# Routing of the first half sequence in five stages less, and a thinner first turn of experts

## The chip, the cores and the metric

The kernel runs on one core of a Trainium2 chip. The metric is the device time of one execution in microseconds; the time before is 976.54, the median of three executions (974.52, 976.54 and 977.25). The engines are named as the profile names them: PE (TensorE, with its weight loads as PEld), DVE (VectorE), ACT (ScalarE), POOL (GpSimd) and SP, which issues most DMAs.

## The reference, cut to what matters

Four sequences of 1024 tokens with 256 channels pass a linear attention with 16 heads, and then a mixture of eight experts. Each token takes its two best experts; each expert takes at most 320 tokens of a sequence, in token order, so the place of a token depends on how many tokens before it chose the same expert.

```python
x = x + attn(layernorm(x))                       # 16 heads of 16, recurrent state over chunks
h = layernorm(x)
probs = softmax(h @ gate_w.T)                    # 8 experts
_, chosen = top_k(probs, 2)
count = cumsum(one_hot(chosen), axis=tokens)     # per sequence and expert
kept = count <= 320                              # the capacity of one expert in one sequence
x = x + sum over kept of probs * (silu(h @ w1[e]) * (h @ w3[e])) @ w2[e]
```

## The kernel before, in words

**Blocks and stages.** The attention goes over 16 blocks of 256 tokens, four to a sequence. For each block the loop at L1091 runs 15 stages; every stage advances a few generators by one step, so one stage is a small piece of PE work. I count the stages through: stage 58 is the thirteenth of the fourth block. `front` makes the projections of a block one to two blocks ahead, `chunk` the scores (tile `pa`, masked by DVE into `aw`) and the outputs (tile `y`) of 128 tokens, `back` the group normalisation (a chain of DVE instructions on `var`, `rah`, `ryh`), the gate (`zT`) and the output projection (`po`), which DVE adds to `x`.

**Order.** PE keeps the order in which the program issues (`manual_schedule`). The other engines' queues are ordered by a scheduler that works from its own estimates. Each queue runs strictly in its order.

**Routing.** When half a sequence of 512 tokens has gone through `back`, the generator `routed` is put in line. Each stage advances it by two steps, so a step that yields without work delays what follows by half a stage. `logits` normalises the rows into the tile `hs`, transposes them on PE (`trh`), multiplies by the gate (`pl`), transposes the result back (`plt`) and copies it to `lg`. `route` picks the two experts by small DVE instructions on 128x32 elements (`mx`, `d`, `cand`, `sel`), adds up the choices within a partition (`before`, L742), lets PE add over partitions and count (the two matmuls of `pcnt`, L751 and L754), and makes the row numbers `is` and the weights in `hs` by some fifteen more small DVE instructions (L758 to L809). Then POOL scatters the rows of `hs` to a buffer `disp` in DRAM, one DMA of 128 rows at a time (L815): eight for the first half sequence. Segment 0 is the first half of sequence 0, segment 1 its second half, segments 2 to 4 whole sequences.

**Experts.** The expert work is a generator `work` that yields after each small piece and tells how many columns it streamed. There are four turns of eight experts. In the first turn every expert has one tile of 128 rows, all from segment 0; it may begin `LAGS[0]` = 8 stages after segment 0 is routed. An expert loads its weights and its rows `xe` from `disp` (SP, L863), transposes them (`pe`, L884), makes seven hidden pieces (`p`, L915, then ACT's silu and DVE's product `act`, L904), and the result (`pw`, L936), which POOL adds to the output in DRAM (L943). After each stage a credit grows by `RATES[turn]` columns, and expert pieces are issued until it is used up.

**Constants.** Stages 1 to 240 carry attention. After them only experts remain. `AFTER` = (0, 2, 3, 4) tells which segment must be routed before each turn. POOL also computes `xx` (L407), a part of the mixes `xm_g` (L453, L457) and the recurrent state (L559, L561), all in the same queue as the scatters.

Of the kernel before, what the change touches and what calls it, by code (L numbers as in the profile page):

```python
# [40 lines left out]
AFTER = (0, 2, 3, 4)  # L41
# [9 lines left out]

FIRST = 5

RATES = (455, 1470, 1400, 1400)

LAGS = (8, 5, 4, 4)

# [8 lines left out]
def rwkv_then_moe_kernel(  # L66
# [24 lines left out]
    def bank(tag, name):  # L91
        return ps.tile(
            [P, 512], F32, tag=tag, name=name, bufs={"m": 4, "y": 1, "f": 3}[tag])
# [12 lines left out]
    def rows(ap, b, r):  # L106
        i = b * T + r * RB
        return ap[i:i + RB, :].rearrange("(t p) c -> p t c", p=P)
# [220 lines left out]
    def norm_stats(key, src, nm, t0=0, n=RT, behind=None, by_rows=False):  # L329

        ve = sm.tile([P, n], F32, tag=f"ve{n}", name=f"ve{nm}", bufs=2)
        nb = sm.tile([P, n], F32, tag=f"nb{n}", name=f"nb{nm}", bufs=2)
        if by_rows:
            st = sm.tile([P, n, 6], F32, tag="st", name=f"st{nm}", bufs=2)
            mv = sm.tile([P, n, 2], F32, tag="mv", name=f"mv{nm}", bufs=2)
            for t in range(n):
                nc.vector.bn_stats(st[:, t, :], src[:, t0 + t, :])
                nc.vector.bn_aggr(mv[:, t, :], st[:, t, :])
                yield
            mean, sign = mv[:, :, 0], -1.0  # L340
            nc.vector.tensor_scalar(ve, mv[:, :, 1], LN_EPS, ROOT, ALU.add, ALU.mult)
        else:

            mean, sign = sm.tile([P, n], F32, tag="mn", name=f"mn{nm}", bufs=2), 1.0
            for t in range(n):
                with tc.issue_after(behind) if behind else nullcontext():
                    nc.scalar.activation(  # L347
                        aside, src[:, t0 + t, :], AF.Copy, scale=-1.0 / C,
                        accum_out=mean[:, t:t + 1])
                nc.scalar.activation(  # L350
                    aside, src[:, t0 + t, :], AF.Square, bias=mean[:, t:t + 1],
                    accum_out=ve[:, t:t + 1])
                yield
            nc.vector.tensor_scalar(ve, ve, ROOT / C, LN_EPS * ROOT, ALU.mult, ALU.add)
        rs, parts = rsqrt(ve, n, nm)
        parts[0]()
        yield
        parts[1]()
        last["nb"] = nc.vector.scalar_tensor_tensor(
            nb, mean, sign, rs, ALU.mult, ALU.mult).ins  # L360
        stats[key] = rs, nb, t0
# [5 lines left out]
    def normed(dst, src, key, t):  # L367
        rs, nb, t0 = stats[key]
        t -= t0
        return nc.scalar.activation(  # L370
            dst, src, AF.Identity, bias=nb[:, t:t + 1], scale=rs[:, t:t + 1])
# [245 lines left out]
    def segment_of(b, r):  # L617
        return next(g for g, (sb, t0, nt) in enumerate(SEGMENTS)
                    if sb == b and t0 <= r * RT < t0 + nt)

    def logits(b, r):

        nm = f"{b}_{r}"
        nc.sync.dma_start(out=rows(out, b, r), in_=xb[b, r])
        yield from norm_stats(("f", b, r), xb[b, r], f"f{nm}")
        yield
        hs = a2.tile([P, RT, W], F32, tag="hs", name=f"hs{nm}")
        nc.gpsimd.iota(
            hs.bitcast(I32)[:, :, C:C + 1], pattern=[[P, RT], [0, 1]], base=b * T + r * RB,
            channel_multiplier=1)  # L630
        for t in range(RT):
            normed(hs[:, t, :C], xb[b, r][:, t, :], ("f", b, r), t)
            if t == TPB - 1:
                yield
        g = segment_of(b, r)
        t0 = r * RT - SEGMENTS[g][1]
        if t0 == 0:
            last["hs"] = []
            last["lg"] = sm.tile([P, SEGMENTS[g][2], E], F32, tag="lg", name=f"lg{g}", bufs=2)
        last["hs"].append(hs)  # L640
        yield from (None,) * (6 if g < AFTER[1] else 2)

        hTs = []
        for u in range(RT // TPB):
            pt = bank("m", f"trh{nm}_{u}")
            for cc in range(CC):
                for i in range(TPB):
                    nc.tensor.transpose(
                        pt[:, cc * TB + i * P:cc * TB + (i + 1) * P],
                        hs[:, u * TPB + i, cc * P:(cc + 1) * P], ident)  # L650
            hT = a1.tile([P, CC, TB], F32, tag="hT", name=f"hT{nm}_{u}", bufs=2)
            nc.scalar.copy(hT.rearrange("p cc i -> p (cc i)"), pt)
            hTs.append(hT)
            yield
        yield from (None,) * 3
        pl = bank("m", f"pl{nm}")
        for cc in range(CC):
            for t in range(RT):
                u, i = divmod(t, TPB)
                nc.tensor.matmul(  # L660
                    pl[32 * t:32 * t + 32, :P], gt[:, cc, :], hTs[u][:, cc, i * P:(i + 1) * P],
                    start=cc == 0, stop=cc == CC - 1, tile_position=(0, 32 * t),
                    skip_group_check=True,
                )
        lgT = sm.tile([P, P], F32, tag="lgT", name=f"lgT{nm}")
        nc.scalar.copy(lgT, pl[:, :P])
        yield from (None,) * 3
        pg = bank("m", f"plt{nm}")
        nc.tensor.transpose(pg[:, :P], lgT, ident)
        nc.scalar.copy(  # L670
            last["lg"][:, t0:t0 + RT, :],
            pg[:, :P].rearrange("p (t e) -> p t e", t=RT)[:, :, :E])
        yield from (None,) * 2

    def route(g):
# [70 lines left out]
                earlier[:, 1:, :], earlier[:, 1:, :],  # L746
                last["earlier"].unsqueeze(1).to_broadcast([P, nt, E]), ALU.add)
        last["earlier"] = earlier[:, nt, :]
        yield from (None,) * (2 if g == AFTER[-1] else 8)
        pc = bank("m", f"pcnt{nm}")  # L750
        nc.tensor.matmul(  # L751
            pc[:, :(nt + 1) * E], ones, flat(earlier), start=True, stop=False,
# [264 lines left out]
    def routed(b, r):  # L1017
        yield from logits(b, r)
        g = segment_of(b, r)
        if (r + 1) * RT == SEGMENTS[g][1] + SEGMENTS[g][2]:  # L1020
            yield from route(g)
            clock.routed[g] = clock.step
# [67 lines left out]
    with tc.manual_schedule(engines={ENG.PE}):  # L1090
        for n in range(NBLK):  # L1091
# [13 lines left out]
            for i, stage in enumerate((  # L1105
# [19 lines left out]
                clock.step += 1  # L1125
                credit = min(credit + RATES[clock.turn], 4 * RATES[clock.turn])

# [74 lines left out]
```

## Time and profile before

| | |
|---|---|
| median of three executions | 976.54 us (974.52 to 977.25) |
| the profiled execution | 978.46 us, of which the span on the core is 976.7 us |
| PE busy | 944.2 us (97%) |
| DVE busy | 447.0 us (46%), but 18.47 of 20 us at 80 to 100 us |
| ACT, POOL busy | 320.1 us (33%), 244.6 us (25%) |
| mean granted PE clock | 0.988 |

A row of the windows view gives, for a stretch of time in us, the busy time of PE, PEld, DVE, ACT and POOL with the number of instructions, then the granted PE clock, the share of DMA and the GB/s. A row of the timeline gives start, duration, engine, source line, operation, tiles and count; the square bracket holds the idle time before it and what ended it. All times count from the start of the span.

### The profile page before, as it was taken

The numbers are of one execution on the slowest core, as the hardware profiler recorded it, in microseconds if no ns is written. First come the engines' busy times: TensorE is split into PE (matmuls) and PEld (weight loads), VectorE is DVE, ScalarE is ACT, GpSimd is POOL, SyncE is SP. The second block draws the span as 40 slices with busy tenths as digits, with TensorE's granted clock in tenths as the row PEclk, the third lists the DMA queues.
The fourth block names the chain that finished last, engine by engine and source line by source line (L and its number), as shares of the span: only waits on it lengthen the run. The fifth ranks groups of instructions, "written<-read, shape, count | busy, mean of one in ns | idle before, by whom it ended". The sixth has DMA issues, their size and how long they took to land. (4 is left out here: it accounts for less than half of the span.)

```text
span 976.7 us, 17096 instructions
## 1 busy us (share of the span) xinstructions
PE 944.2 (97%) x6754; PEld 749.7 (77%) x6754; DVE 447.0 (46%) x1303; ACT 320.1 (33%) x811; POOL 244.6 (25%) x265
## 2 busy tenths in 40 slices
PE   7989899999999999999999999999999999999995
PEld 6766678878787788888788778888866866767664
DVE  7888766656676634445443434322221222222221
ACT  8647544743654531524214124111111111111110
POOL 5321513312227212121452111541111110211111
PEclk9999999989999999999999999999999999999998
DMA  5997224514446444353465545785645234433421
GB/s 162 245 252 244 84 95 142 184 60 141 153 125 219 153 124 136 93 153 89 128 192 151 153 135 157 208 248 168 175 123 153 76 87 147 135 94 92 147 54 19
DMA packets 92073, 139.06 MB, mean 142 GB/s; under 512 B 5456, under 2 KB 73552, under 8 KB 91984
## 3 DMA queue, kind: packets, MB, share of 16 engines
q1 hardware_dynamic: 79120, 120.36, 39.2%
q0 software_dynamic: 12720, 17.47, 9.7%
q8 instruction: 58, 0.95, 0.4%
q14 instruction: 31, 0.25, 0.1%
q10 hardware_dynamic: 144, 0.02, 0.0%
HBM read 103.45 MB, written 34.39 MB: 141 GB/s over the span
## 5 line engine op out<-in xcount | busy, mean ns | idle before, releaser
L915 PE MATMUL p<-xeT,w 128*128 128x256 f32 (+2 forms) x1960 | 430.8, 374 | 2.8 <-DVE act L904 1.5
L915 PEld LDWEIGHTS p<-xeT,w 128*128 128x128 f32 x1960 | 328.4, 191 | 94.8 <-issue 10.5
L920 ACT ACTIVATE sl<-p 128x256 f32<-128x256 f32 (+2 forms) x245 | 91.2, 375 | 486.6 <-PE p L915 479.1
L904 DVE TENSOR_TENSOR act<-sl,p 128x256 f32<-128x256 f32 (+2 forms) x245 | 99.5, 408 | 284.2 <-ACT sl L920 168.4
L943 POOL DMA_INDIRECT y_out<-ye,xe x67 | 105.3, 1571 | 478.0 <-DVE ye L940 448.1
L936 PE MATMUL pw<-w,act 128*128 128x256 f32 x938 | 211.9, 381 | 0.3 <-DVE act L904 0.3
L936 PEld LDWEIGHTS pw<-w,act 128*128 128x128 f32 x938 | 174.9, 190 | 24.6 <-DVE act L904 1.0
L940 DVE TENSOR_SCALAR ye<-pw,xe 128x256 f32<-128x256 f32 x67 | 32.1, 483 | 138.6 <-PE pw L936 138.5
L510 DVE TENSOR_TENSOR aw<-pa,wmat 128x512 f32<-128x512 f32 x128 | 79.4, 683 | 11.4 <-PE pa L502 11.3
L815 POOL DMA_INDIRECT disp<-hs,is x64 | 63.7, 996 | 44.3 <-issue 15.4
L423 PE MATMUL pc<-xm,wa 128*128 128x256 f32 x264 | 67.1, 400 | 5.9 <-DVE aw L510 3.1
L423 PEld LDWEIGHTS pc<-xm,wa 128*128 128x128 f32 x264 | 50.2, 198 | 16.2 <-DVE aw L510 3.7
L413 DVE SCALAR_TENSOR_TENSOR xm<-xx,ch,xT 128x256 f32<-128x256 f32 x98 | 43.5, 479 | 8.5 <-PE pc L423 5.1
L502 PE MATMUL pa<-rT,kT 32*128 32x256 f32 x512 | 43.1, 410 | 2.0 <-DVE rbT L443 1.1
L531 PE MATMUL y<-aw,vpad 128*32 128x128 f32 x1024 | 40.5, 278 | 0.0
L347 ACT ACTIVATE aside<-x 128x256 f32<-128x256 f32 x62 | 25.7, 415 | 37.8 <-DVE x L615 37.0
L502 PEld LDWEIGHTS pa<-rT,kT 32*128 32x128 f32 x512 | 26.5, 187 | 11.2 <-issue 3.4
L610 PE MATMUL po<-wa,zT 128*128 128x256 f32 x128 | 30.7, 383 | 4.1 <-DVE zT L602 2.6
L531 PEld LDWEIGHTS y<-aw,vpad 128*32 128x32 f32 x1024 | 24.4, 109 | 12.2 <-issue 11.7
L464 PE MATMUL pt<-wa,xm 128*128 128x256 f32 x128 | 32.2, 397 | 0.9 <-DVE rbT L443 0.9
L407 POOL TENSOR_TENSOR xx<-xT 128x512 f32<-128x512 f32 x15 | 15.7, 1049 | 67.2 <-ACT xT L401 67.2
L610 PEld LDWEIGHTS po<-wa,zT 128*128 128x128 f32 x128 | 23.5, 190 | 7.9 <-ACT xT L393 2.8
(184 smaller groups left out, 797.3 us busy)
## 6 DMA issues: line engine op xcount, KB each, us to landing
w<-w_in SPq DMA_DIRECT2D x96, 896.0 KB, 6.4
disp<-empty SPq DMA_DIRECT2D x8, 795.0 KB, 15.4
disp<-empty SPq DMA_DIRECT2D x16, 265.0 KB, 9.5
xe<-disp SPq DMA_DIRECT2D x16, 265.0 KB, 2.9
xe<-disp SPq DMA_DIRECT2D x8, 530.0 KB
y_out<-x SPq DMA_DIRECT2D x8, 512.0 KB, 3.3
x<-x_in SPq DMA_DIRECT2D x7, 512.0 KB, 4.3
wa<-w_attn_in SPq DMA_DIRECT2D x5, 256.0 KB, 4.9
```

The costliest lines, as they stand in the source:

```text
L413: last["xm"] = nc.vector.scalar_tensor_tensor(xm[:, cc, :], xx[:, cc, :], maa(m, cc), xT[:, cc, 1:TB + 1], ALU.mult, ALU.add,).ins
L423: nc.tensor.matmul(pp[:, m * TB:(m + 1) * TB], wa[w][:, cc, m * P:(m + 1) * P], xm[:, cc, :], start=cc == 0, stop=cc == CC - 1,)
L502: nc.tensor.matmul(pa[g][:, cc * TB:(cc + 1) * TB], o.kT[rows32, cc, cols], o.rT[rows32, cc, :, cols], start=True, stop=True, tile_positio ...
L510: nc.vector.tensor_tensor(w.rearrange("p q i -> p (q i)"), pa[g], wmat[:, 4 * g:4 * g + 4, :].rearrange("p q i -> p (q i)"), ALU.mult,)
L531: nc.tensor.matmul(y[32 * g:32 * g + 32, :], o.vp[:, t, cc * 4 + g, q * 32:(q + 1) * 32], aw[g][:, cc * 2 + q, :], start=state is None and ...
L610: nc.tensor.matmul(po[:, t * C:(t + 1) * C], zT[:, cc, t * P:(t + 1) * P], wa[W_O][:, cc, :], start=cc == 0, stop=cc == CC - 1,)
L815: ins = nc.gpsimd.indirect_dma_start(out=disp[:, :], out_offset=bass.IndirectOffsetOnAxis(ap=idx_s[g][:, c, t:t + 1], axis=0), in_=last["h ...
L904: nc.vector.tensor_tensor(act, sl, p3[:, :w], ALU.mult)
L915: nc.tensor.matmul(pp[:, :w], wt[:, cc, f * P:(f + 1) * P], xeT[:, cc, lo:lo + w], start=cc == 0, stop=cc == CC - 1,)
L920: nc.scalar.activation(sl, p1[:, :w], AF.Silu)
L936: nc.tensor.matmul(po[:, :C], acts[f][:, i * P:(i + 1) * P], w2e[:, f, :], start=f == 0, stop=f == FC - 1,)
L943: ins = nc.gpsimd.indirect_dma_start(out=out[:, :], out_offset=bass.IndirectOffsetOnAxis(ap=xe.bitcast(I32)[:, t, C:C + 1], axis=0), in_=y ...
```

## The change

Three constants change, all for segment 0 and the turn that depends on it. In `logits`, segment 0 now yields two empty steps instead of six before its transposes (two stages less). In `route`, segment 0 now yields two instead of eight before the count matmuls (three stages less). The credit of the first turn grows by 420 columns a stage instead of 455. Segments 1 to 4 keep their steps.

```diff
-RATES = (455, 1470, 1400, 1400)
+RATES = (420, 1470, 1400, 1400)
...
         last["hs"].append(hs)
-        yield from (None,) * (6 if g < AFTER[1] else 2)
+        yield from (None,) * (6 if 0 < g < AFTER[1] else 2)
...
         last["earlier"] = earlier[:, nt, :]
-        yield from (None,) * (2 if g == AFTER[-1] else 8)
+        yield from (None,) * (2 if g in (0, AFTER[-1]) else 8)
         pc = bank("m", f"pcnt{nm}")
         nc.tensor.matmul(
             pc[:, :(nt + 1) * E], ones, flat(earlier), start=True, stop=False,
```

## The prediction

> **What bounds the kernel now.** I read the page first, then the windows at 5 us, then the timelines of PE, DVE and POOL where the windows show holes.
>
> ```profile
> span 976.7 us, 17096 instructions
> PE 944.2 (97%) x6754; PEld 749.7 (77%) x6754; DVE 447.0 (46%) x1303; ACT 320.1 (33%) x811; POOL 244.6 (25%) x265
> ```
>
> PE is the bound: 32.5 us of the span are not PE. The change adds and removes no matmul, so it can only change PE's idle time and the time at half clock. The windows show where those are:
>
> ```profile
> 105.00:110.00 5.00, 3.63 (x26) 2.92 (x25) 3.92 (x9) 2.20 (x6) 4.06 (x6) 1.00 0.31 108
> 115.00:120.00 5.00, 2.68 (x14) 1.85 (x14) 4.21 (x17) 4.94 (x15) 0.74 (x3) 0.77 0.58 182
> 120.00:125.00 5.00, 5.00 (x26) 3.72 (x25) 2.25 (x6) 3.55 (x13) 2.13 (x2) 0.55 0.36 110
> 195.00:200.00 5.00, 3.86 (x76) 2.63 (x79) 4.36 (x16) 2.04 (x4) 1.94 (x2) 0.96 0.87 284
> 200.00:205.00 5.00, 5.00 (x26) 3.95 (x25) 2.77 (x5) 0.28 (x1) 0.11 (x1) 0.50 0.12 31
> 315.00:320.00 5.00, 3.54 (x24) 2.91 (x20) 2.88 (x6) 4.91 (x13) 3.56 (x5) 1.00 0.31 110
> ```
>
> The first number after the length is PE's busy time, the number before the DMA share is the granted clock. There are two dips to half clock, after the holes at 115-120 and 195-200; by the clock's share in these rows and their neighbours each lasts some 6.8 us. A like hole at 315-320 brought none. The chain around the first dip:
>
> ```profile
> 96.18 0.19 DVE L742 TENSOR_TENSOR before<-sums 128x32 f32<-128x32 f32 x1
> 98.09 0.31 PE L751 MATMUL pcnt<-before,ones 128*128 128x40 f32 x2
> 103.11 1.27 POOL L815 DMA_INDIRECT disp<-hs,is  x1 [2.52 <-DVE off L763]
> 109.77 1.04 POOL L407 TENSOR_TENSOR xx<-xT 128x512 f32<-128x512 f32 x1
> 113.78 0.96 POOL L815 DMA_INDIRECT disp<-hs,is  x1 [0.30 <-issue]
> 118.57 3.78 PE L423 MATMUL pc<-xm,wa 128*128 128x256 f32 x8 [1.65 <-DVE aw L510]
> 122.14 0.63 PE L884 MATMUL pe<-ident,xe 128*128 128x128 f32 x2
> ```
>
> PE counts at 98.09, POOL scatters from 103.11 to 114.7, and PE has its first expert work at 122.14. Until then only attention runs, and DVE is nearly full. The pc at 118.57 ran at half clock: 3.78 us, where the same eight matmuls take 1.99 elsewhere.
>
> **The change part by part.** The built program gives the new queue orders, the trace of before the durations.
>
> *1. Transposes and logits two stages earlier.* `trh` moves to just before and after `y` of stages 51 and 52. Its PE time (0.66 + 0.60) is only moved. PE idles 0.86 at 83.58 before (for DVE's rbT), so this hole takes some of it; but the next `po` waits for `zT`, which DVE ends at 89.7 either way. Gain 0. The new DVE order puts `mx` right behind `zT`, at 89.9 rather than 90.47. DVE is busy from 89.87 to 96.48 in both, so `before` ends only some 0.3 us earlier than 96.37: at 96.1.
>
> *2. Count three stages earlier.* `pcnt` moves ahead of `y`, `pa` and the `pc` of K, that is from 98.09 to the end of the gate's `pc`, 93.40 (91.51 + 1.89). Its input comes at 96.1. So PE, in its strict order, waits about 2.7 us, with the outputs `y`, the scores `pa` and thus `aw` behind it. This is a new wait.
>
> *3. The small instructions L758 to L809.* Before, they stand between those of the rsqrt chain, whose own pitch (0.33 us) hardly changes: they are free. Now they stand alone before `aw`: from 96.8, fifteen at 0.1 to 0.2, to 98.7. `aw` then starts at 99.5, when `pa` is there, not at 96.48: 3.0 later. The rsqrt chain behind it is shorter without them (before 99.37 to 104.39, where one `got` took 1.11 us against 0.21 for the same size in L791): about 102.0 to 106.0. So the delay falls to 1.6 at the next `aw`; PE's `y`, `pt`, `trx`, `prs` behind the delayed count make it 2.2 again at `zT`. `po` starts at 110.3 (before: 108.07), after a wait of 0.7 rather than 1.37.
>
> *4. Scatters on POOL.* They start at 99.1, 4.0 earlier. The pitch is 1.28 (103.11 to 109.49 for five). Six run, to 106.8; then `xm_g`, which stands before all of them in the old order, takes 2.2 (1.04 + 0.07 + 1.09), to 109.0; then two more, to 111.6. The gate's `pc` that needs `xm_g` comes at 112.1, so that is covered by 3 us. `xx`, queued behind the last two, comes at 112 instead of 109.77 and delays the mixes by as much as everything else is late: no more. Landing: the last scatter before was issued at 113.78 and the `xe` load at 116.39, 2.6 later; now 110.3 + 2.6 = 112.9, and a load of this size takes 2.2 (page, part 6): rows at 115.3 with the wait's overhead. SP's queue has only the second `xe` load moved ahead of one store of x. That store and the next x load slip by under 1 us (0.50 for the issue at 117.27): their users are over 20 us away. If that cover were gone, 0.5.
>
> *5. Experts five stages earlier.* The first is begun at stage 73 instead of 78. PE reaches its transposes at 110.3 + 1.83 + 1.89 = 114.0 and waits 1.3 to 1.5 for the rows. Then expert pieces fill the holes that before had.
>
> *6. The rate.* The first turn is 8 x (7 x 512 + 128 + 7 x 256) = 44,032 columns: 96.8 stages at 455, 104.8 at 420. Eight longer, five earlier: in the built order the second turn's first expert begins at stage 171 rather than 172, and from stage 175 on the expert matmuls issued differ by at most 8 at any stage. Work shifted within a full PE costs nothing, and the second turn covers the rest; if not, one expert result, 3.2 us (189.20), would be bare. One more table load on ACT (32 for 31, 1.28 us) lies beside an engine at 33%. POOL's first add to the output (1.57) now stands before a state update rather than behind; its `ye` is done several us earlier than the update's input: 0, or 1.6.
>
> **The sum, 89.7 to 137 us, in PE time lost.** Before: 1.37 (po), 0.07 + 0.67 (pa), 1.65 (pc), the dip (half of the 6.0 us in which PE works at half clock: 3.0), 1.18 (p at 127.98), 0.76 (trh at 136.66): 8.7. After, if the clock stays full: 2.7 (count), 0.7 (po), 1.4 (rows), and for waits on `act` and silu about 1.0 (estimate, from the 1.18 of before): 5.8. Gain 2.9.
>
> But does the clock stay full? The rows: the dips of before come after 1.45 to 1.7 us of idle time in about 3.4 us, and after 1.14 at 198.29 among small matmuls; 1.46 at 316.39 brought none. The Trainium skill, "TensorE: Matmul & The Clock Gate", sections "What's actually happening" and "Why this matters for your kernels", says that the clock falls to half after an idle window of about 3.4 us, that the windows run freely, and advises against gaps over about 3 us. By that rule the count's wait, 2.7, is below the limit, and the gain stays 2.9. By the rows it is far more idle than what brought a dip, so one comes at about 97: 3.4 lost, of which the wait for the rows (1.4) is absorbed, since they come at 115.3 whatever PE does. Gain 2.9 - 2.0 = 0.9. I take the rows. The page's limit alone would not give the dips that the trace has.
>
> The second dip: its place (`y` and `pa` of the block's sixth and seventh stages with no expert piece beside them, after a result `pw`) is filled after the change; but stages 94 to 97, the same place one block earlier, are now bare (before: 4, 4, 2 and 7 matmuls). It may go (gain 1.14 + 3.4 = 4.5), stay as a like dip 14 stages earlier, or come twice. Likeliest: a like dip, 0.
>
> The profiled execution took 978.46, 1.9 above the median and above all three runs shown; 978.46 - 0.9 = 977.6, and on the median's scale 976.54 - 0.9 = 975.6. If the median runs lack one of the two dips, the gain turns into a loss of about 2.
>
> **The rivals.**
> - *Full clock at the count* (the page's rule holds, or the idle time straddles two windows): 976.5 - 2.9 = 973.6. For: one hole of 1.46 without a dip. Against: two with less idle time that had one.
> - *The second dip vanishes*: with a moved first dip 975.6 - 4.5 = 971.1, without 969.1. For: the expert pieces at stages 111 and 112. Against: the bare stages 94 to 97.
> - *Slower: the new count wait costs two dips.* The place is stages 58 to 66, where DVE is nearly full (18.47 of 20 us), so PE at half clock delays `pa`, DVE idles, and the next stretch is thin too; with another dip at 94 to 97 beside the old one, three in place of two. Price: 3.4 on top of the moved one, and the count's wait 1 us longer if `before` ends at 97: 975.6 + 4.4 = 980. It decides from the point where the delay at `zT` exceeds about 5 us (2.2 + 3.4 by my sum: just there).
> - *Nothing moves*: the rows of experts are late by POOL and DVE, and the start is worth what the count's wait costs: 976.5.
>
> **How the numbers follow.** Moved dip 0.36 (975.6), nothing 0.08, full clock 0.18 (973.6), second dip gone 0.14 (970), slower 0.24 (980). The measurement tells about 0.3%, 2.9 us, from no change: 973.6 to 979.5. Of the full-clock case half falls under it, of the moved dip a tenth on either side. So faster 0.14 + 0.09 + 0.04 = 0.27, slower 0.24 + 0.04 + 0.01 = 0.29, the same 0.44. The range leaves out the far ends of the outer cases: 969.5 to 981. The likeliest case alone: 973.5 to 978.
>
> **What would show it right or wrong.** PE's `pcnt` with 2 to 3.5 us of idle time before it, released by DVE L742 or L738; the first scatter at 99, the last before 112; the wait of `pe` for `xe` under 2 us; first expert piece at about 115 instead of 123; a clock under 0.8 in 95 to 105 and full in 117 to 125; the row 195 to 205 at full clock, and perhaps 155 to 170 not. A count without a wait, or a dip in three places, would make it wrong.

## The result, and the profile after

The changed kernel took 979.63 us (median of 16 executions, 977.27 to 981.33), the kernel before 977.26 beside it (16 executions, 974.52 to 979.29): a ratio of 1.003, 95% interval 1.002 to 1.004. A second series gave 980.54 against 976.49: 1.0036 (1.0021 to 1.0052). So the change costs some 2.4 to 4 us. The predicted 975.6 was on the wrong side, and the rival "slower" (980) is what happened.

The profiled execution of the changed kernel took 977.27 us, the fastest of its 16. The profiled one of before took 978.46, slower than its median. Read against each other, the two profiles show a small gain, and the medians a loss. Both have to be explained.

The page of after, its first lines, then the windows view (columns as before):

```profile
span 975.5 us, 17105 instructions
PE 941.6 (97%) x6754; PEld 748.3 (77%) x6754; DVE 448.8 (46%) x1303; ACT 321.6 (33%) x812; POOL 245.4 (25%) x265
```

```profile
95.00:100.00 5.00, 3.10 (x40) 1.88 (x44) 3.44 (x24) 2.22 (x8) 0.25 (x1) 0.72 0.00 0
110.00:115.00 5.00, 3.14 (x19) 2.30 (x19) 5.00 (x12) 2.31 (x6) 2.76 (x5) 0.92 0.17 58
115.00:120.00 5.00, 5.00 (x26) 3.95 (x24) 2.83 (x7) 1.29 (x5) 0.70 (x1) 0.74 0.26 82
200.00:205.00 5.00, 4.52 (x32) 3.28 (x31) 4.31 (x12) 0.56 (x2) 0.32 (x1) 1.00 0.11 30
315.00:320.00 5.00, 4.15 (x30) 3.75 (x28) 2.97 (x6) 4.91 (x17) 2.28 (x3) 1.00 0.25 85
```

PE has a new hole and a new dip in 95-100 (clock 0.72), and a second hole at 110-115 with a dip into 115-120 (0.92 and 0.74). By the clock's records the dips are 97.2 to 100.6 and 114.2 to 117.6, 3.4 us each, where before had 6.8 us from 117.7 and 6.8 us from 199.6. The dip at 200 is gone. The timeline, in the order of time:

```profile
96.57 0.19 DVE L742 TENSOR_TENSOR before<-sums 128x32 f32<-128x32 f32 x1
96.90 0.39 PE L751 MATMUL pcnt<-before,ones 128*128 128x40 f32 x2 [2.73 <-DVE before L742]
99.75 1.18 POOL L815 DMA_INDIRECT disp<-hs,is  x1 [9.69 <-DVE hs L809]
106.57 0.29 DVE L322 SCALAR_TENSOR_TENSOR rah<-ryh 128x128 f32<-128x128 f32 x1
106.89 1.72 DVE L323 TENSOR_TENSOR rah<-rah,var 128x128 f32<-128x128 f32 x1
107.40 1.05 POOL L453 TENSOR_TENSOR xm_g<-xx,ch 128x512 f32<-128x512 f32 x1
108.53 1.09 POOL L457 TENSOR_TENSOR xm_g<-xm_g,xT 128x512 f32<-128x512 f32 x1
108.64 1.12 DVE L324 SCALAR_TENSOR_TENSOR rah<-rah 128x128 f32<-128x128 f32 x1
110.63 0.67 DVE L510 TENSOR_TENSOR aw<-pa,wmat 128x512 f32<-128x512 f32 x1
111.08 0.97 POOL L815 DMA_INDIRECT disp<-hs,is  x1 [0.30 <-issue]
114.30 3.62 PE L610 MATMUL po<-wa,zT 128*128 128x256 f32 x8 [1.65 <-DVE zT L602]
119.48 0.38 PE L884 MATMUL pe<-ident,xe 128*128 128x128 f32 x2
```

The count waits 2.73 us. The scatters start at 99.75 and end at 112. Then two instructions of the rsqrt chain take 1.72 and 1.12 us instead of 0.29, each until just after POOL's instruction beside it has ended (108.61 after 108.45, 109.76 after 109.62). The next `aw` comes at 110.63 and `po` at 114.30, 6.2 us later than before (108.07), and `po` runs at half clock. The first expert transposes, at 119.48, wait for nothing: PE is later than the rows.

The same place before. There POOL's mix `xm_g` stretched only one small instruction, `got`, and the rsqrt chain has its usual lengths:

```profile
99.50 1.09 POOL L457 TENSOR_TENSOR xm_g<-xm_g,xT 128x512 f32<-128x512 f32 x1
99.57 1.11 DVE L785 TENSOR_TENSOR got<-sel,held 128x64 f32<-128x64 f32 x1
103.05 0.29 DVE L323 TENSOR_TENSOR rah<-rah,var 128x128 f32<-128x128 f32 x1
104.39 2.48 DVE L510 TENSOR_TENSOR aw<-pa,wmat 128x512 f32<-128x512 f32 x4
108.07 1.97 PE L610 MATMUL po<-wa,zT 128*128 128x256 f32 x8 [1.37 <-DVE zT L602]
```

The starts of `po`, which each block issues once, show where the difference of the two profiles arises. The second series' profile of the same changed kernel stands beside it ("again"), and two of the experiments below. Values are us later (+) or earlier (-) than in the profile of before, where that block's `po` starts at the time in the first column. The first row stands ahead of the first instruction that the change moves: the second profile and E7 are late there already, since they have 6.8 us of half clock from 11 us on where before and after have 3.4. Of before itself there is only this one profile.

| `po` before, at us | after | after, again | E7, mix on DVE | E9, filler and mix |
|---|---|---|---|---|
| 69.0 | 0.0 | +0.7 | +0.6 | +0.1 |
| 108.1 | +6.2 | +7.0 | +5.9 | +3.2 |
| 146.0 | +3.2 | +4.7 | +1.2 | -0.4 |
| 175.8 | +2.6 | +4.1 | +0.6 | -0.9 |
| 212.9 | -2.0 | -0.6 | -4.0 | -5.6 |
| 305.5 | -3.4 | -2.0 | -5.4 | -7.0 |
| 346.9 | -1.3 | +2.3 | -1.2 | -2.9 |
| last matmul, 966.8 | -1.3 | +2.6 | -0.5 | -2.3 |

One correction belongs to it: until the first turn ends, the changed kernels have issued another amount of expert work: 420 columns a stage from stage 73 against 455 from stage 78, that is 4,830 - 35 x stage columns more. At 146 us (stage 86) that is 1.8 us more, at 305 (about stage 161) 0.8 us less, by the 5.10 us that 40 matmuls of 128 columns take at 121.76. So at 146 the profiled after had lost 1.4 us and the other 2.9, of which 0.7 is from the first row. Between 176 and 213 both gain 4.6 to 4.7 by the table, of which 0.5 is again the amount of work: the old second dip with its wait of 1.14 does not come. At 305 to 347 the profiled one loses 2.1, of which 0.8 is the expert work it had still to do, and the other 4.3, so 1.3 and 3.5 without it. The difference is a dip, as the windows of the second profile show:

```profile
310.00:315.00 5.00, 3.35 (x57) 2.29 (x55) 3.54 (x18) 4.75 (x11) 3.94 (x4) 0.97 0.62 213
315.00:320.00 5.00, 5.00 (x22) 4.00 (x22) 2.97 (x6) 4.96 (x13) 3.57 (x5) 0.50 0.30 109
```

```profile
314.38 2.66 PE L502 MATMUL pa<-rT,kT 32*128 32x256 f32 x12 [1.65 <-ACT gT L490]
```

PE waits 1.65 us for ACT's `gT` and then runs at half clock for 6.8 us, 3.4 lost. The profiled after waited 1.48 there and kept its clock, though E8 with 1.18 did not. The five other profiles with both moves and the rate of 420 (E5 to E9) all have a dip that begins between 309 and 314. So the profiled after is the exception, and in the others the second dip is not gone: it has moved from 200 to 313.

### The profile page after: what moved, and what is told of

It reads as the page before. It is cut to its first block, busy times and chain, and to the rows that moved or that the text cites. A ratio compares the mean times of both kernels' runs of the same rounds, so it can differ in the third digit from the quotient of the medians.

```text
span 975.5 us, 17105 instructions
## 1 busy us (share of the span) xinstructions
PE 941.6 (97%) x6754; PEld 748.3 (77%) x6754; DVE 448.8 (46%) x1303; ACT 321.6 (33%) x812; POOL 245.4 (25%) x265
## 5 line engine op out<-in xcount | busy, mean ns | idle before, releaser
L904 DVE TENSOR_TENSOR act<-sl,p 128x256 f32<-128x256 f32 (+2 forms) x245 | 99.5, 407 | 278.6 <-ACT sl L920 162.6
```

The lines of the kernel that those rows point to most:

```text
L904: nc.vector.tensor_tensor(act, sl, p3[:, :w], ALU.mult)
```

## The experiments

All ratios are to the kernel before in the same series, with 95% intervals. The series stand apart: in the first (E1 to E4) the kernel before took 988.8 us and in the last (E13 to E15) 990.1, in the others 976.3 to 976.5. Numbers of these two series compare only within themselves.

### First series: the parts at other sizes

E1, the rate alone (`RATES` begins with 420).

> Only the rate of the first turn goes from 455 to 420; the routing keeps its stages. Theory 1 (what costs is the new wait of PE at the count matmuls, with the dips of the clock behind it): the median stays within 1 us of before, about 977.5, since PE is full from stage 80 on and the first expert is at the same stage. Theory 2 (what costs is the thinner filling of the attention stages by expert pieces): slower by 2 us or more, about 979.5, with more short waits of PE between 150 and 330 us. The second turn begins four stages later than before, which theory 2 makes dearer than in the changed kernel.

E2, the count alone.

> Only the count matmuls of segment 0 come three stages earlier (two empty steps for eight); rate 455, logits as before. Theory 1: PE waits 2.5 to 3.3 us before the count, a dip follows at 97 to 101, and the median is 2 to 3.5 us above before: about 980. Theory 2: no loss, the start of the experts three stages earlier gives up to 1 us: 976.5.

```diff
-        yield from (None,) * (2 if g == AFTER[-1] else 8)
+        yield from (None,) * (2 if g in (0, AFTER[-1]) else 8)
```

E3, the logits alone.

> Only the transposes and logits of segment 0 come two stages earlier; the count keeps its eight empty steps, rate 455. Theory 1: no wait at the count (its input is ready 0.5 us earlier than before and the count stands after the scores), the median is between 975.5 and 977.5. Theory 2: the same or a little faster, since the rate is unchanged: 976. A slow result here, 979 or more, would speak against both: then the earlier start of the experts itself costs.

```diff
-        yield from (None,) * (6 if g < AFTER[1] else 2)
+        yield from (None,) * (6 if 0 < g < AFTER[1] else 2)
```

E4, both moves with the rate of 455.

> Both moves of the routing as in the changed kernel, but the rate stays at 455. Theory 1: as slow as the changed kernel, 979 to 980.5, with a wait of 2.7 us at the count. Theory 2: the loss is gone, 976 to 977.5.

Measured: E1 0.9972 (0.996 to 0.9984), E2 0.9972 (0.996 to 0.9985), E3 1.0063 (1.0044 to 1.0083), E4 1.0028 (1.0016 to 1.0039). With the old rate the second turn begins earlier (stage 169 or 170), and its first transposes wait for rows: 6.9 us at 322 in E4, 2.3 in E2, 1.1 in E3. So in this series only the two moves together speak for a lower rate; E2 was faster than before all the same. At the count E2 waited 1.27 us, not the 2.5 to 3.3 expected, and E4 waited 2.73 as the changed kernel does, but kept full clock behind it; its dip came at 110.5. More is not to be had from a series where before itself took 12 us more.

### Second series: the count's wait and POOL's mix

The changed kernel again.

> The changed kernel itself beside the kernels of this group, on one chip, so that they can be compared with each other. Both theories: 0.2 to 0.3% over before, with a wait of 2.7 us at the count; on a chip like that of the group before, where the rows of experts land later, perhaps a wait at the first transposes of the second turn too.

Measured: 1.0036, as told above.

E5, the changed kernel with the distance of the count cut by one stage instead of three, and the experts still begun at the same stage.

> The changed kernel, but the count stands two stages later (six empty steps instead of two) and the first turn may begin six stages after the routing instead of eight, so that experts begin at the same stage as in the changed kernel. Theory 1 (the wait at the count and its dip cost the time): the wait goes from 2.7 to under 1 us, the dip at 97 goes, and the median falls 1.5 to 3 us below the changed kernel's, to no more than before. The rows of experts come 1 to 3 us later, which may show as a wait at the first transposes. Theory 2 (the thin rate): as slow as the changed kernel, within 1 us.

```diff
-LAGS = (8, 5, 4, 4)
+LAGS = (6, 5, 4, 4)
...
-        yield from (None,) * (2 if g in (0, AFTER[-1]) else 8)
+        yield from (None,) * (2 if g == AFTER[-1] else 6 if g == 0 else 8)
```

E6, the changed kernel with ten matmuls of `ones` ahead of the count, into the same bank, which the count then overwrites.

> The changed kernel with ten matmuls of 128x128 more ahead of the count, into the same bank, which the count then overwrites; they fill the wait (2.6 us at 0.26 each) without shortening it. If the half clock behind the wait is what costs: no dip at 97 to 101, and 1 to 2 us below the changed kernel. If only the wait itself costs: the same time as the changed kernel within 0.5 us, or slower by what the ten matmuls overrun.

```diff
         pc = bank("m", f"pcnt{nm}")
+        if g == 0:
+            for _ in range(10):
+                nc.tensor.matmul(pc[:, :P], ones, ones, start=True, stop=True, skip_group_check=True)
```

E7, the changed kernel with the mix `xm_g` of that one block on DVE instead of POOL.

> The changed kernel, but the gate's mix of one block (second block of sequence 1) is made by DVE instead of POOL, where it lies among the scatters. In the changed kernel's trace two instructions of the rsqrt chain beside that POOL work took 1.72 and 1.12 us, where 0.29 is usual. If that is contention of the two engines and it lies on the path: those two rows are back at 0.29, DVE does two instructions of 0.5 us more, zT is 1 to 2 us earlier, the rows of experts land 2 us earlier, and the median is 0.5 to 2 us below the changed kernel's. If not: no difference.

```diff
-        if b == 0 and blk == 0:
+        if b == 0 and blk == 0 or b == 1 and blk == 1:
             xm_g = mixed(MIX_G)
```

Measured: E5 1.0007 (0.9995 to 1.0019), E6 1.0008 (0.9997 to 1.0018), E7 1.0006 (0.9997 to 1.0015). Each takes the whole loss away or all but a trace of it, 3.6 to 4.2 us by the medians and more than was forecast, and in different ways. E5 and E6 keep the stretched rsqrt instructions (1.72 and 1.12 us in E5, one of 1.85 in E6); E7 keeps the count's wait and the dip behind it, but not the second dip (114 to 120). Means over the executions separate them: the span times the mean granted clock is about what the span would be at full clock (an estimate, since idle time inside a dip counts half).

| | mean us | mean clock | span x clock |
|---|---|---|---|
| before | 976.21 | 0.9907 | 965.39 |
| after, again | 979.47 | 0.9894 | 967.34 |
| E5, count later | 976.71 | 0.9925 | 967.65 |
| E6, filler | 976.70 | 0.9925 | 967.60 |
| E7, mix on DVE | 976.86 | 0.9901 | 965.51 |

The change costs 1.95 us of the last column and 0.0013 of clock, which is 1.3 us of the span: 3.3 together. E5 and E6 give the clock back and 0.0018 more, and no waiting time: what the earlier `aw` gains there, PE loses in a new wait of 1.9 to 2.0 us for `act` at 120 to 123. E7 gives back the waiting time (1.83) and half of the clock (0.0007). It also takes 2.2 us of work from POOL's queue, so that the last scatter starts 2.0 us earlier (109.43 for 111.47); but in the second profile of the changed kernel neither PE's transposes nor DVE's mixes waited for POOL, so the gain there is not from that. The windows of E6 at the count show the dip gone (0.72 in after), though PE streams ten matmuls for nothing; below it its count, its first `aw`, and its rsqrt instruction beside POOL's mix:

```profile
95.00:100.00 5.00, 4.59 (x78) 3.55 (x80) 3.50 (x24) 2.85 (x10) 0.44 (x1) 1.00 0.01 3
96.88 0.41 PE L754 MATMUL pcnt<-before,ones 128*128 128x40 f32 x2 [0.41 <-DVE before L742]
100.45 2.48 DVE L510 TENSOR_TENSOR aw<-pa,wmat 128x512 f32<-128x512 f32 x4 [1.19 <-PE pa L502]
106.58 1.85 DVE L325 SCALAR_TENSOR_TENSOR ryh<-rah,ryh 128x128 f32<-128x128 f32 x1
```

### Third series: both remedies, and the controls

E8 is E5 with E7's edit.

> Both remedies together: the later count (six empty steps, lag 6) and the gate's mix of one block on DVE. If the count's dip and the contention with POOL are separate losses of the changed kernel, each worth 2.5 to 4 us there, they add: the time goes below before, by 1.5 to 3 us (about 974 where before is 976.5), with the product of span and clock near that of the kernel with the mix on DVE, and the mean clock near that of the one with the later count. If they are two ways to the same loss, the time is that of either alone, equal to before.

E9 is E6 with E7's edit.

> The filled count wait and the gate's mix of one block on DVE. As for the kernel before it in this group: 1.5 to 3 us below before if the two losses are separate; equal to before if they are one.

E10 is the kernel before with E7's edit alone.

> The kernel before with the gate's mix of that one block on DVE, nothing else. If the contention is a matter of the change (the mix lies beside the rsqrt chain only there; before, one instruction of 1.11 us instead of 0.21 suffers): within 1 us of before. If the mix on DVE is simply better anywhere: 1.5 to 2.5 us faster than before, and then its gain in the changed kernel says nothing of the change.

E4b runs E4 again.

> The changed kernel with the rate of 455, on this group's chip. On the chip of the first group it lost 0.28%, with a wait of 6.9 us at the first transposes of the second turn, which begins at stage 169 there and at 171 in the changed kernel. If the rate's use is only to keep the second turn from beginning early: where rows land as early as in the profile of before, no such wait, and the time of the changed kernel within 1.5 us. If the thin rate costs: 2 us less than the changed kernel.

Measured: E8 0.9988 (0.9975 to 1.0001), E9 0.9982 (0.9974 to 0.999), 975.41 us against 976.31, E10 1.0006 (0.9998 to 1.0014), E4b 1.0085 (1.0072 to 1.0098). By these ratios E6 gained 0.28% on the changed kernel and E7 0.30%; together, in E9, 0.54%, so the two losses come near to adding up. Against before that leaves 0.18%, at the low end of the forecast (E8: 0.12%, not clear of noise). So E9 is faster than both kernels by a little, and it is not because the mix is better on DVE: before gains nothing from that. The DVE timeline of E9 has the rsqrt instructions at their usual length, and `aw` 3.1 us earlier than in after (110.63):

```profile
105.86 0.29 DVE L322 SCALAR_TENSOR_TENSOR rah<-ryh 128x128 f32<-128x128 f32 x1
106.19 0.29 DVE L323 TENSOR_TENSOR rah<-rah,var 128x128 f32<-128x128 f32 x1
107.53 0.68 DVE L510 TENSOR_TENSOR aw<-pa,wmat 128x512 f32<-128x512 f32 x1
```

Of the 3.1 us, 0.7 had been gained before the chain's second L322 (105.86 for 106.57), and the rest is the stretch. E4b confirms what the rate is for with both moves. Its PE timeline, and POOL's queue at that place:

```profile
329.10 1.11 PE L884 MATMUL pe<-ident,xe 128*128 128x128 f32 x4 [7.67 <-DMA xe<-disp]
```

```profile
318.75 1.61 POOL L943 DMA_INDIRECT y_out<-ye,xe  x1 [2.06 <-issue]
319.77 0.95 POOL L561 TENSOR_TENSOR state<-state,upd 128x64 f32<-128x64 f32 x1
320.89 1.00 POOL L815 DMA_INDIRECT disp<-hs,is  x1 [0.17 <-issue]
322.19 0.97 POOL L815 DMA_INDIRECT disp<-hs,is  x1 [0.30 <-issue]
```

The second turn asks for rows whose last two scatters stand on POOL behind an expert's output add. The change without the thinner rate is the slowest version of its series.

### Fourth and fifth series: the parts alone

E1b runs E1 again.

> Only the rate, 455 to 420, once more, since the group in which it ran first took 12 us more for before than every other group. Theory 1 (the routing's move costs, by its dip and by the work beside POOL): within 1 us of before. Theory 2 (the thin rate costs): 2 us slower. The second turn's first expert is at stage 176 instead of 172; if that costs, slower by up to 1 us.

E11 is the count alone with a rate of 440, E12 the logits alone with a rate of 444: the second turn then begins at stage 172 as before.

> Only the count three stages earlier (logits as before), with a rate of 440, which puts the second turn's first expert at stage 172 as before. The count stands behind the outputs y and ahead of the scores pa; PE waits there about 1.3 us (as in the first group), and the gate's mix on POOL stands among the scatters. Theory 1: a part of the loss of the changed kernel, 1 to 3 us over before, with a dip near 97 in most executions. Theory 2: within 1 us of before.

> Only the transposes and logits two stages earlier, with a rate of 444, which puts the second turn's first expert at stage 172 as before. The count stands behind the scores, and the gate's mix on POOL ahead of all scatters, as before. Theory 1: no wait at the count, no long instructions in the rsqrt chain; the first experts two stages earlier give 0 to 1.5 us below before. If it is slower by 2 us or more, the earlier start of experts itself costs, and theory 1 is not the whole cause.

Measured: E1b 1.0011 (1.0002 to 1.002), E11 1.0042 (1.0029 to 1.0056), E12 1.0043 (1.003 to 1.0056). E12 has no wait at the count, has `xm_g` ahead of the scatters and the rsqrt chain at its usual length (one small instruction, `tmp`, takes 0.95 us beside the mix, as `got` took 1.11 in before), and still lost 3.5 us. By its own forecast that speaks against theory 1 as the whole cause. Its profile has dips at 109.5, 119.7 and 317.7 instead. In E11's profile the count's wait of 1.27 us brought no dip, against the forecast; it has a wait of 2.11 us for `zT` at 273 that no other profile has. So a single part at a rate fitted to it has losses of its own, and they can't be read as shares of the change's loss.

E13 and E14 are these two with the rate of the change, 420, and E15 is the rate of 444 alone.

> The kernel before with the move of the logits and the rate of 420, the count at its old distance. The same move with a rate of 444 took 3.5 us more than before. If that loss belongs to starting the routing two stages earlier, about 980 again. If it belongs to the rate of 444 (to where the expert pieces then stand against the attention), this one stands between the rate alone (0.9 over before) and both moves with a later count (0.1 under): 976 to 978. Full clock at the count, no wait there.

> The kernel before with the move of the count and the rate of 420, the logits at their old distance. With a rate of 440 it took 3.5 us more than before, of which 2.9 us of PE waits at 250 to 274 us. If the count's wait of 1.3 and POOL's mix beside the rsqrt chain are the loss, 978.5 to 980 with any rate. If those later waits, which belong to the rate, were most of it, 976.5 to 978.

> The kernel before with a rate of 444 in the first turn and nothing else. If the position of the expert pieces at this rate is what cost the logits move its 3.5 us, 978 to 980; if the rate is harmless, within 1.5 us of before: 975.5 to 978.

Measured against 990.09: E13 1.0007 (0.9996 to 1.0018), E14 0.9932 (0.9912 to 0.9951), E15 1.0003 (0.9991 to 1.0014). Taken by their ratios, E13 falls on the side where the logits move by itself costs nothing, E15 on the side where the rate of 444 costs nothing, and E14 gains 6 us, which no theory had. But the kernel before takes 13.6 us more in this series than in the fourth: E15, which differs from it by 11 columns a stage, is 9.7 us behind the first profile of before at the `po` of 347 us, where the kernels with the rate of 420 are 2 to 3 ahead. So what E14 gains there may be a part of this extra loss that it escapes. What lengthens every kernel in the first and the last series stays open (the chip alone is not it: by the record the first and the third series ran on the same one), and so does why E12 loses 3.5 us in the fourth.

## Why the prediction was wrong, point by point

**The transposes (step 1): not free.** They were to cost nothing, because the next `po` waits for `zT` at 89.7 either way. But `pa` now waits 1.15 us for ACT's copy `hT`, and `po` comes 0.8 us later; the first line is before, the others after:

```profile
89.71 1.97 PE L610 MATMUL po<-wa,zT 128*128 128x256 f32 x8
84.08 1.15 PE L502 MATMUL pa<-rT,kT 32*128 32x256 f32 x16 [1.15 <-ACT hT L652]
90.48 1.97 PE L610 MATMUL po<-wa,zT 128*128 128x256 f32 x8 [0.83 <-DVE zT L602]
```

Every profile with this move has 21.5 us from the preceding `po` to this one, every profile without it 20.7.

**The count (step 2): right.** The wait is 2.73 us for the predicted 2.7, with the right releaser, though it ends 0.8 us late (96.90 for 96.1). By the limit in the Trainium skill, "TensorE: Matmul & The Clock Gate", section "Why this matters for your kernels", no idle gaps over some 3 us, no dip was due; by the rows one was. Four of the five profiles with this wait have it (at 97.2 in the profiled run and 99.7 in the second, in E7 and in E4b), and E4 has not. In the first three it lasted 3.4 us, half of the 6.8 that the prediction's 3.4 lost would need. With the wait filled to 0.41 us (E6) or cut to 0.88 (E5) it doesn't come: the dip needs the wait, but the wait does not always bring it.

**The small instructions and the delay (step 3): the step that failed.** Predicted were a delay of 3.0 at the first `aw`, 1.6 at the next and 2.2 at `zT`. Measured were 5.4 (101.89 for 96.48), 6.2 (110.63 for 104.39) and 6.2 (`po` at 114.30). At the second `aw` 4.6 us are missing, and three terms make them up. The first: I took `pa` to be there at 99.5; in E6, with the clock full, `aw` starts at 100.45 and still waits 1.19 us for `pa`, 1.0 later, of which 0.8 is step 1. The second: I let the dip cost 3.4 on PE and forgot DVE, which waits for the `y` and `pa` that PE now computes at half clock: 1.4 more (101.89 for 100.45). The third and largest: two instructions of the rsqrt chain grew by 1.43 and 0.83 us beside POOL's mix `xm_g`, 2.3 together, a term that the prediction put at nothing. Step 4 had the mix at 106.8 to 109.0, and step 3 had the chain end at 106.0, so on paper they just missed each other; with the chain 2.4 us late, and the mix at 107.40 to 109.62, they met. The Trainium skill, "SBUF — State Buffer", sections "Who interferes with whom" and "Summary: rules for kernel authors", has the rule: a VectorE instruction with both inputs in SBUF and a GpSimd instruction that reads SBUF contend, and the one that comes second waits for the other's end. The ends here agree to 0.16 us. One thing doesn't: L323's row begins 0.5 us ahead of POOL's, and it lost all the same. I had the row for it in hand, `got` with 1.11 us against 0.21 in before, and did not ask what stood beside it: the same mix. Of the mix, step 4 asked only whether the gate's `pc` has to wait for it.

**The scatters and the rows (steps 4 and 5): nearly right.** From 99.75 and to 111.08, for 99.1 and 110.3 predicted. The wait for the rows of 1.4 did not come, because PE was 5.5 us later at its transposes than predicted (119.48 for 114.0). The first hidden piece starts at 121.76, not at about 115.

**The first stretch as a sum.** It was to gain 0.9 and lost 1.4 in the profiled run, 2.9 in the second, or 2.2 without the late start of that run. The slower rival named its own condition: two dips at the count once the delay at `zT` exceeds about 5 us. The delay was 6.2 and 7.0, and there were two dips, at 97 to 100 and 114 to 117 (116.7 in the second). Its other dip, at stages 94 to 97, did not come: these bare stages kept full clock.

**The second dip.** I took "moves, change 0" as the likeliest, and that holds for its size but not its place: it is at 313, behind ACT's `gT`, in six of seven profiles with the rate of 420 and both moves. In the profiled after it vanished, the -4.5 of the rival. In the profiles with the rate alone (E1 and E1b) there is no dip at 200 either, so its going needs no moved routing. Together, with the amount of work taken out: in the second profile +2.9 (start), -4.2 (dip at 200 gone) and +3.5 (wait and dip at 313) make 2.2 of the 2.6 us that it ends later than before's profile, in the profiled one +1.4, -4.1 and +1.3 make the small gain.

**The scale.** I moved a difference between two profiles onto the median by subtraction, and warned that before's profile held more than its typical run. The sum met the profiled time (977.6 predicted, 977.27 measured) with a failed step and a vanished dip that cancel: a single profiled execution confirmed a wrong sum. In the second series, before took a median 978.0 at a mean clock of 0.988 and 974.2 at 0.993, so how long an execution runs at half clock moves it by as much as the change does.

**The rate (step 6).** Alone it costs about 1 us (E1b, 1.0011, with 1.0002 the low end; E1, in the lengthened first series, was 0.3% faster) where I had it at nothing. That both moves need it E4b shows.

## What to carry to other kernels

When a change moves work on a queue that isn't the bound, draw what now runs beside it on the other engines: here POOL's mix came to lie beside a DVE chain and stretched it, and taking it away was worth 1.8 us of waiting time by the estimate above. Allow for lateness in the drawing: here the two missed each other only if the chain was on time. A wait that brings a dip is paid twice, on PE and again on the engine that waits for PE's half-speed results; here, where the wait stayed, matmuls for nothing in it were cheaper than the dip. And where the number of dips differs from run to run, compare two or three profiles of each kernel before any sum is put on a median.

## What the runs showed of the hardware

Dips came in lengths of 3.4 and 6.8 us, in E3, E4b and E15 also of 10.2, and idle time of the same size did not always bring one: 2.73 us at the count brought one in four profiles and none in E4; at 312, 1.48 us brought none in the profiled after, 1.65 did in the second profile, and 1.18 did in E8. Ten matmuls without a use, some 2.4 us of PE, made the kernel 0.4% faster (976.52 for 980.54), all of it by the clock (mean 0.9925 for 0.9894). And the same instruction of 128x128 elements took 0.29 us or 1.72 us by what POOL did at the time, where the scatters that POOL issued beside the other 0.29 us instructions stretched none of them.
